# Turning the next routed tile's rows during the present tile, and dealing the sorted tiles out over three places of weights

## The chip, the cores and the metric

One core of a Trainium2 chip runs the whole program in one launch. The metric is the device time in microseconds (us); lower is better. Each time is that of one execution; the median of several is given.

## The reference, cut to what matters

The input is 64 sequences of 128 rows of 256 numbers (fp32). A state-space layer and a decayed cross attention, each followed by a layer norm, give rows x2. What matters here is the last part, a mixture of experts, and its layer norm:

```
shared = (silu(x Wg0) * (x Wu0)) Wd0                    # every row
probs  = sigmoid(x R + b); two experts of eight per row, scores s1, s2
out    = layernorm(x + shared + s1*expert_e1(x) + s2*expert_e2(x))
expert_e(x) = (silu(x Wg[e]) * (x Wu[e])) Wd[e]         # 256 -> 512 -> 256
```

There are 8192 rows, so 16384 pairs of a row and an expert. Which experts a row goes to depends on the data.

## The kernel before, in words

The rows are taken in 16 groups of 512. For each group, first_half (front and scan: the state-space layer), second_half (after: attention; route: the router) and the shared expert follow on each other. Work of different groups is interleaved by a planner that runs while the program is written: abreast (L1236) holds generators and always takes the step that is furthest behind; placed (L1254) gives a generator its place in time; a yielded number is the work of TensorE, in estimated us, that should pass before the generator goes on. work[0] counts that work (L535). The tile layer then orders each engine's instructions by readiness under these priorities, so an engine's order is fixed in the program, but need not be the order in which the source issues them.

**Routing.** route writes each row twice, with its destination and its score, into a table xs in HBM, in the region of its expert (indirect DMAs from GpSimd, POOL in the profile, L992). In five places tile_list (L1039) makes a list of tiles from the counts so far. BATCHES (L41) gives the number of tiles and rows: 9, 16, 16, 16 tiles of 256 rows after 4, 8, 12 and 16 groups, and 21 tiles of 128 rows at the end, 78 in all. The list is sorted by expert: position p of a batch holds the p-th tile of the sorted sequence. An entry holds the expert, the first row in xs, and a flag that says whether the expert differs from that of the tile three positions earlier.

**A routed tile.** There are three places of weights, routed_w0 to routed_w2 (1.5 MB each: gate, up and down of one expert); tile i uses place i % 3 (NW = 3). fetch (L1134) copies the list's entry (L1139, POOL), then SP reads it, loads the rows (rows_in, L1142) and, if the flag is set, the weights (L1148); the instruction waits for the place to be free and stands in SP's order also where it skips the transfer. SP carries many other DMAs in order. refill (L1121) fetches up to three tiles ahead; there[i] is the planned time at which tile i is ready, 12 us after its fetch.

one_tile (L1204) waits for there[i], runs hidden (L1156), then down (L1187) of the tile before, then refills. hidden transposes the rows on TensorE (four turns of 128 x 128 for 256 rows, two for 128), copies them from PSUM to rows_T on ScalarE (ACT, L1166), copies the row destinations `to` (L1168) and scores `wt` (L1170) on POOL, and yields 1.2. Then follow the products of gate and up in PSUM tiles gu (three buffers, shared with the shared expert), silu on ACT (L1182) and the multiply on VectorE (DVE, L1183) into hid: two rounds for 256 rows, one for 128. down makes the product with the third matrix, scales it (L1196) and scatters the rows to ys (L1197, indirect DMA of POOL; it reads `to`). The buffers: rows_in 3, rows_T 2, to and wt 3, hid 4, rows_out 2.

**The end.** After the last group the remaining tiles run (other_tiles, L1445), beside fill_behind (L1100), which writes filler rows behind each expert's region (8 indirect DMAs on POOL, 7 DMAs on SP, L1115), and the last shared expert. Then come the shared experts of seven groups and, for every group, combine: x2 plus the two rows of ys, layer norm, output.

All matmuls go through product (L536, the matmul at L543), transposes through turn (L545, L547), so the profile shows them under these lines, told apart by their tiles. One fp32 matmul shows as two MATMUL records, a transpose as one.

Of the kernel before, what the change touches and what calls it, by code (L numbers as in the profile page):

```python
# [11 lines left out]
F32 = mybir.dt.float32  # L12
AF = mybir.ActivationFunctionType
ALU = mybir.AluOpType
# [5 lines left out]
KD = D // P  # L20
# [7 lines left out]
NE = 8  # L28
# [8 lines left out]
NW = 3  # L37
# [3 lines left out]
BATCHES = [(4, 0, 9, 256), (8, 9, 16, 256), (12, 25, 16, 256), (16, 41, 16, 256), (16, 57, 21, 128)]  # L41
NT = sum(n for _, _, n, _ in BATCHES)
DX = D + 2
MOST = max(n for _, _, n, _ in BATCHES)
# [456 lines left out]
def shared_decay(K):  # L501

    with ExitStack() as ctx:
        _shared_decay(ctx, K)


def _shared_decay(ctx, K):  # L510
    tc, nc = K.tc, K.tc.nc
# [10 lines left out]
    const = ctx.enter_context(tc.tile_pool(name="masks", bufs=1))  # L522
# [12 lines left out]
    work = [0.0]  # L535

    def product(out, lhsT, rhs, **how):
        n = 1
        for size in rhs.shape[1:]:
            n *= size  # L540
        tiled = P // lhsT.shape[-1] if "tile_position" in how else 1
        work[0] += 2 * max(0.00084 * n, 0.11 if n > 64 else 0.06) / tiled
        nc.tensor.matmul(out, lhsT=lhsT, rhs=rhs, **how)  # L543

    def turn(out, src, ident):  # L545
        work[0] += 0.11
        nc.tensor.transpose(out, src, ident)  # L547
# [39 lines left out]
    def project(ps, w, col, src):  # L587

        for k in range(KD):
            product(  # L590
                ps, lhsT=w[:, k, col : col + P], rhs=src[:, k, :],
                start=(k == 0), stop=(k == KD - 1),
            )
# [445 lines left out]
    def tile_list(k):  # L1039

        groups, first, n, size = BATCHES[k]
        last = k == len(BATCHES) - 1
        d = done[k]
        pn = pm.tile([P, NE], F32, name="pm")
        product(pn, lhsT=ones, rhs=count, start=True, stop=True)
        if last:
            behind = small.tile([P, NE], F32, name="behind", bufs=1)
            nc.vector.tensor_tensor(behind, pn, behind0, ALU.add)  # L1050
            nc.vector.tensor_copy(behind_i, behind)

        def tiny(name, shape=(P, NE)):
            return small.tile(list(shape), F32, name=name, bufs=1)


        nt_f = tiny("nt_f")
        nc.vector.tensor_scalar(nt_f, pn, float(size - 1) if last else 0.0, None, ALU.add)
        nt_i = small.tile([P, NE], mybir.dt.int32, name="nt_i", bufs=1)
        nc.vector.tensor_copy(nt_i, nt_f)  # L1060
        nc.vector.tensor_scalar(nt_i, nt_i, size.bit_length() - 1, None, ALU.arith_shift_right)
        upto_e = tiny("upto_e")
        nc.vector.tensor_copy(upto_e, nt_i)
        nt = tiny("nt")
        nc.vector.scalar_tensor_tensor(nt, d, -1.0 / size, upto_e, ALU.mult, ALU.add)
        cum2 = tiny("cum2", (P, NE, NE))
        nc.vector.tensor_tensor(cum2, bef, nt.unsqueeze(1).to_broadcast([P, NE, NE]), ALU.mult)
        cum0 = tiny("cum0")
        nc.vector.tensor_reduce(cum0, cum2, AX.X, ALU.add)
        if not last:  # L1070
            more = tiny("more")
            nc.vector.tensor_scalar(more, cum0, -1.0, float(n), ALU.mult, ALU.add)
            nc.vector.tensor_scalar(more, more, 0.0, None, ALU.max)
            nc.vector.tensor_tensor(more, more, nt, ALU.min)
            nc.vector.scalar_tensor_tensor(done[k + 1], more, float(size), d, ALU.mult, ALU.add)
        cum = tiny("cum", (1, NE))
        nc.vector.tensor_tensor(cum, cum0[0:1], nt[0:1], ALU.add)

        skip = tiny("skip", (1, NE))
        nc.vector.tensor_scalar(skip, upto_e[0:1], -float(size), float(CAP), ALU.mult, ALU.add)  # L1080
        nc.vector.tensor_tensor(skip[:, 0 : NE - 1], d[0:1, 1:NE], skip[:, 0 : NE - 1], ALU.add)
        ge = small.tile([1, MOST, NE], F32, name="ge", bufs=1)[:, 0:n, :]
        nc.vector.tensor_tensor(
            ge, number[:, 0:n].unsqueeze(2).to_broadcast([1, n, NE]),
            cum.unsqueeze(1).to_broadcast([1, n, NE]), ALU.is_ge,
        )
        mine = ex[:, NW + first : NW + first + n]
        nc.vector.tensor_reduce(mine, ge, AX.X, ALU.add)
        nc.vector.tensor_scalar(mine, mine, float(NE - 1), None, ALU.min)
        nc.vector.tensor_tensor(ge, ge, skip.unsqueeze(1).to_broadcast([1, n, NE]), ALU.mult)  # L1090
        row = small.tile([1, MOST], F32, name="row", bufs=1)[:, 0:n]
        nc.vector.tensor_reduce(row, ge, AX.X, ALU.add)
        nc.vector.scalar_tensor_tensor(row, number[:, 0:n], float(size), row, ALU.mult, ALU.add)
        wh = what[:, first : first + n, :]
        nc.vector.tensor_scalar(wh[:, :, 0], mine, 1.0, None, ALU.add)
        nc.vector.tensor_scalar(wh[:, :, 1], row, d[0:1, 0:1], None, ALU.add)
        nc.vector.tensor_tensor(wh[:, :, 2], mine, ex[:, first : first + n], ALU.not_equal)
        known[0] = first + n
# [20 lines left out]
    ahead, room = [], [NW]  # L1119

    def refill():  # L1121

        while fetched[0] < min(room[0], known[0]):
            ahead.append(fetch(fetched[0]))
            there.append(work[0] + 12.0)
            fetched[0] += 1

    fetched, there = [0], []

    def shape(i):  # L1130

        return next((k, size) for k, (_, first, n, size) in enumerate(BATCHES) if i < first + n)
# [20 lines left out]

    listed, waiting = [0], []

    def hidden(i, t):  # L1156
        _, size = shape(i)
        w = weights[i % NW]
        wg = w[:, 0:SZ].rearrange("p (k i) -> p k i", k=KD)
        wu = w[:, SZ : 2 * SZ].rearrange("p (k i) -> p k i", k=KD)  # L1160
        ps = pm.tile([P, KD, size], F32, name="pm")
        for k in range(KD):
            for j in range(size // P):
                turn(ps[:, k, j * P : (j + 1) * P], t[:, j, k * P : (k + 1) * P], ident)
        tT = tiles.tile([P, KD, size], F32, name="rows_T", bufs=2)
        nc.scalar.copy(tT, ps)  # L1166
        to = tiles.tile([P, size // P], mybir.dt.int32, name="to", bufs=3)
        nc.gpsimd.tensor_copy(to, t[:, :, D])  # L1168
        wt = tiles.tile([P, size // P], F32, name="wt", bufs=3)
        nc.gpsimd.tensor_copy(wt, t[:, :, D + 1])  # L1170
        yield 1.2
        hid = []
        each = T // size
        for c0 in range(0, CF, each):
            psg = gu.tile([P, each, size], F32, name="gu")
            psu = gu.tile([P, each, size], F32, name="gu")
            for ps, w2 in ((psg, wg), (psu, wu)):
                for c in range(each):
                    project(ps[:, c, :], w2, (c0 + c) * P, tT)
                yield  # L1180
            hc = tiles.tile([P, each, size], F32, name="hid", bufs=4)
            nc.scalar.activation(hc, psg, AF.Silu)  # L1182
            nc.vector.tensor_tensor(hc, hc, psu, ALU.mult)  # L1183
            hid += [hc[:, c, :] for c in range(each)]
        return hid, to, wt

    def down(i, hid, to, wt):  # L1187
# [16 lines left out]
    def one_tile():  # L1204

        i = listed[0]
        listed[0] += 1
        refill()
        yield max(0.0, there[i] - work[0])
        made = yield from hidden(i, ahead.pop(0))  # L1210
        if waiting:
            yield from down(*waiting.pop())
        waiting.append((i, *made))

        room[0] = i + NW
        refill()
        yield
# [98 lines left out]
    for half in (L // 2, L // 4, L // 8):  # L1316
        t = const.tile([P, L // half, half], F32, name=f"middle{half}")
        n = L // half
# [6 lines left out]
    for side in range(2):  # L1325
        t = one.tile([P, KB // NS, NS], F32, name=f"half{side}", tag="dm")
# [3 lines left out]
        while half >= Q:  # L1330
# [7 lines left out]
        tT = const.tile([KB, P], F32, name=f"halfT{side}")  # L1338
# [4 lines left out]
    SZ = KD * FF  # L1343
# [6 lines left out]
                   allow_small_or_imprecise_dtypes=True)  # L1350
# [7 lines left out]
                   allow_small_or_imprecise_dtypes=True)  # L1358
# [8 lines left out]
    behind0 = const.tile([P, NE], F32, name="behind0")  # L1367
    nc.gpsimd.iota(behind0, pattern=[[CAP, NE]], base=0, channel_multiplier=1,
                   allow_small_or_imprecise_dtypes=True)
    number = const.tile([1, MOST], F32, name="number")  # L1370
    nc.gpsimd.iota(number, pattern=[[1, MOST]], base=0, channel_multiplier=0,
                   allow_small_or_imprecise_dtypes=True)
    done = [const.tile([P, NE], F32, name=f"done{k}") for k in range(len(BATCHES))]
    nc.vector.memset(done[0], 0.0)
    ex = const.tile([1, NW + NT], F32, name="ex")
# [3 lines left out]
    weights = []  # L1379
    for i in range(NW):  # L1380
        t = const.tile([P, 3 * SZ], F32, name=f"routed_w{i}")
# [4 lines left out]
                   allow_small_or_imprecise_dtypes=True)  # L1386
# [267 lines left out]
```

## Time and profile before

| | us |
|---|---|
| runs before: median (lowest to highest, 3) | 2053.07 (2049.54 to 2053.74) |
| the profiled execution | 2046.0 |
| its span | 2044.3 |

| group (line, engine, tiles) | instructions or records | busy us | mean ns |
|---|---|---|---|
| gate and up of routed tiles, 256 rows: L543 PE gu<-rows_T,routed_w | 1824 | 432.5 | 388 |
| the same, 128 rows | 672 | 78.7 | 275 |
| down of routed tiles: L543 PE pm<-routed_w,hid | 1080 | 258.4 | 383 |
| transposes of routed rows: L547 PE pm<-ident,rows_in | 270 | 42.4 | 273 |
| multiply of routed tiles: L1183 DVE | 135 | 92.3 | 686 |
| silu of routed tiles: L1182 ACT | 135 | 80.5 | 596 |
| scatter of routed rows: L1197 POOL | 135 | 138.4 | 1026 |

The whole moves 253.60 MB by DMA, and the granted TensorE clock is 0.984 of full. Busy time is the time in which an engine shows an instruction; a wait is idle time put down to what released the engine last, written "engine line <- releaser". PEld is TensorE's weight load, which overlaps its products. Routed tiles run from 380 us to about 1875 us of the span.

### The profile page before, as it was taken

To read this page: it belongs to the slowest core of one execution; us is meant where nothing else is said; L and a number is where in the kernel's file an instruction comes from. 1 tells how busy PE (TensorE), PEld (TensorE's weight loads), DVE (VectorE), ACT (ScalarE), POOL (GpSimd) and SP (SyncE) were. 2 spreads that over 40 slices of the span, in tenths; PEclk is the share of its full clock that TensorE was granted. 3 is DMA by queue.
4 is the path that set the end of the run, shared out by engine and by line. 5 is a ranking of instruction groups with operands and counts; after the bars stand their busy time and mean duration, and the time that the engine had idled before them with its cause. 6 is when DMAs were issued, how large, how long until landed. Compare 5 with 4: busy or idle time off the path is not lost. (4 is left out here: it accounts for less than half of the span.)

```text
span 2044.3 us, 26096 instructions
## 1 busy us (share of the span) xinstructions
PE 1894.9 (93%) x9252; PEld 1396.5 (68%) x9252; DVE 988.5 (48%) x2398; ACT 743.1 (36%) x1239; POOL 462.0 (23%) x697
## 2 busy tenths in 40 slices
PE   4989998999999999999999999998998999999996
PEld 2655666686767676777777676767676888886553
DVE  3667676565555564555555555554431111012574
ACT  3355344344343534353434252534121222221332
POOL 3030221221212122323223121222123222221110
PEclk9899999999999999999999999999999999999998
DMA  4011121422313234333333442433224555862772
GB/s 146 26 54 44 53 64 39 165 90 75 124 44 109 59 135 150 111 126 124 129 121 100 150 140 80 134 116 116 104 80 166 183 184 195 305 218 97 256 268 84
DMA packets 100629, 253.60 MB, mean 124 GB/s; under 512 B 22824, under 2 KB 60328, under 8 KB 91528
## 3 DMA queue, kind: packets, MB, share of 16 engines
q1 hardware_dynamic: 77368, 196.56, 29.1%
q0 software_dynamic: 17616, 52.46, 7.4%
q10 hardware_dynamic: 5504, 2.81, 0.5%
q8 instruction: 75, 1.23, 0.2%
q14 instruction: 66, 0.54, 0.1%
HBM read 207.33 MB, written 58.60 MB: 130 GB/s over the span
## 5 line engine op out<-in xcount | busy, mean ns | idle before, releaser
L543 PE MATMUL gu<-rows_T,routed_w 128*128 128x256 f32 (+1 forms) x2496 | 511.2, 358 | 40.3 <-ACT rows_T L1166 14.8
L543 PEld LDWEIGHTS gu<-rows_T,routed_w 128*128 128x128 f32 x2496 | 421.5, 193 | 115.8 <-issue 34.1
L1183 DVE TENSOR_TENSOR hid<-hid,gu 128x512 f32<-128x512 f32 x135 | 92.3, 686 | 389.4 <-PE gu L543 370.5
L543 PE MATMUL pm<-routed_w,hid 128*128 128x256 f32 x1080 | 258.4, 383 | 9.9 <-DVE hid L1183 9.9
L543 PE MATMUL pm<-xnT,w_in_s 128*128 128x512 f32 x512 | 243.4, 600 | 3.2 <-ACT xnT L580 3.1
L543 PE MATMUL gu<-x2T,shared_w 128*128 128x512 f32 x512 | 230.5, 596 | 3.5 <-DVE hc L1016 2.6
L543 PEld LDWEIGHTS pm<-routed_w,hid 128*128 128x128 f32 x1080 | 198.6, 190 | 51.3 <-DVE hid L1183 14.7
L1197 POOL DMA_INDIRECT ys<-rows_out,to x135 | 138.4, 1026 | 325.5 <-ACT rows_out L1196 252.4
L562 POOL TENSOR_TENSOR rstd<-var,mhalf 128x4 f32<-128x4 f32 x64 | 68.2, 1066 | 508.7 <-DVE mv L558 282.7
L628 DVE SCALAR_TENSOR_TENSOR xc<-pm,cw,xc 128x508 f32<-128x508 f32 (+2 forms) x192 | 141.2, 740 | 77.9 <-ACT xc L623 74.3
L543 PEld LDWEIGHTS gu<-x2T,shared_w 128*128 128x128 f32 x512 | 94.6, 190 | 111.5 <-issue 99.6
L1182 ACT ACTIVATE hid<-gu 128x512 f32<-128x512 f32 x135 | 80.5, 596 | 237.6 <-PE gu L543 217.4
L543 PEld LDWEIGHTS pm<-xnT,w_in_s 128*128 128x128 f32 x512 | 95.6, 193 | 87.2 <-issue 74.1
L567 ACT ACTIVATE x<-x,shift,rstd 128x256 f32<-128x256 f32 x132 | 72.6, 591 | 183.1 <-DVE shift L564 183.1
L543 PE MATMUL pm<-w_out_s,sz 128*128 128x256 f32 x512 | 122.0, 391 | 9.3 <-DVE sz L784 8.3
L1196 ACT ACTIVATE rows_out<-pm,wt 128x256 f32<-128x256 f32 x135 | 57.7, 469 | 199.0 <-PE pm L543 148.5
L543 PE MATMUL gu<-shared_w,hc 128*128 128x256 f32 x512 | 116.7, 382 | 7.3 <-DVE hc L1016 7.3
L543 PEld LDWEIGHTS pm<-w_out_s,sz 128*128 128x128 f32 x512 | 98.5, 195 | 32.9 <-DVE sz L784 14.1
L543 PEld LDWEIGHTS gu<-shared_w,hc 128*128 128x128 f32 x512 | 95.4, 190 | 26.9 <-DVE hc L1016 11.1
L992 POOL DMA_INDIRECT xs<-x,index x64 | 66.9, 1045 | 138.3 <-issue 75.4
L781 DVE SCALAR_TENSOR_TENSOR xc<-xc,dsk,pm 128x512 f32<-128x512 f32 x64 | 47.2, 744 | 84.5 <-PE pm L543 56.3
L623 ACT ACTIVATE xc<-pm,cb,cw 128x512 f32<-128x512 f32 x64 | 49.7, 777 | 105.1 <-PE pm L543 105.1
(233 smaller groups left out, 2465.6 us busy)
## 6 DMA issues: line engine op xcount, KB each, us to landing
routed_w<-in_ffn_dram SPq DMA_DIRECT2D x78, 1536.0 KB
picked<-ys SPq DMA_DIRECT2D x16, 1024.0 KB
rows_in<-xs SPq DMA_DIRECT2D x57, 258.0 KB
cT<-in_ctxT_dram POOLq DMA_DIRECT2D x16, 512.0 KB
cq<-chunks SPq DMA_DIRECT2D x16, 512.0 KB
x_rows<-x SPq DMA_DIRECT2D x16, 512.0 KB
xt<-in_x_dram POOLq DMA_DIRECT2D x10, 512.0 KB
xt<-x_rows SPq DMA_DIRECT2D x10, 512.0 KB
```

The lines of the kernel that those rows point to most:

```text
L543: nc.tensor.matmul(out, lhsT=lhsT, rhs=rhs, **how)
L562: nc.gpsimd.tensor_tensor(rstd, var, mhalf, ALU.pow)
L567: nc.scalar.activation(dst[:, b, :], src[:, b, :], AF.Identity, bias=shift[:, b : b + 1], scale=rstd[:, b : b + 1])
L623: nc.scalar.activation(xcf[:, c, :], ps, AF.Identity, bias=cb[:, c : c + 1], scale=cw[:, c, TAPS - 1 : TAPS],)
L628: nc.vector.scalar_tensor_tensor(xc[:, c, :, s:], ps3[:, :, : L - s], cw[:, c, TAPS - 1 - s : TAPS - s], xc[:, c, :, s:], ALU.mult, ALU.add,)
L781: nc.vector.scalar_tensor_tensor(y, xcf[:, c, :], dsk[:, c : c + 1], ps.rearrange("p b l -> p (b l)"), ALU.mult, ALU.add)
L992: s = nc.gpsimd.indirect_dma_start(out=xs, in_=rows[k][:, b, :], in_offset=None, out_offset=bass.IndirectOffsetOnAxis(ap=index[:, b, k : k ...
L1182: nc.scalar.activation(hc, psg, AF.Silu)
L1183: nc.vector.tensor_tensor(hc, hc, psu, ALU.mult)
L1196: nc.scalar.activation(y[:, j, :], ps[:, j, :], AF.Copy, scale=wt[:, j : j + 1])
L1197: s = nc.gpsimd.indirect_dma_start(out=ys, in_=y[:, j, :], in_offset=None, out_offset=bass.IndirectOffsetOnAxis(ap=to[:, j : j + 1], axis=0),)
```

## The change

Three things change.

The transposes, the copy to rows_T and the copies of `to` and `wt` become a function of their own, rows_turned. hidden of tile i calls it for tile i + 1 after the first round of its own products whose end finds tile i + 1 fetched and planned work within 8 us of there[i + 1] (so 4 us after its fetch), without a yield of its own. A tile whose rows are not turned by then does it itself as before.

The list deals the sorted tiles out: position p of a batch of n holds sorted tile p // 3 + (p % 3) * (n // 3) + min(p % 3, n % 3). So each of the three places of weights gets a contiguous run of the sorted sequence, where before it got every third tile. The flag still says whether the expert differs from that of three positions earlier.

For this the constant row `number` (0, 1, 2, ...) becomes one row for each batch size, made at the start by an iota on POOL and, for 16, two small DVE operations.

```diff
-            ge, number[:, 0:n].unsqueeze(2).to_broadcast([1, n, NE]),
+            ge, numbers[n].unsqueeze(2).to_broadcast([1, n, NE]),
...
-        nc.vector.scalar_tensor_tensor(row, number[:, 0:n], float(size), row, ALU.mult, ALU.add)
+        nc.vector.scalar_tensor_tensor(row, numbers[n], float(size), row, ALU.mult, ALU.add)
...
-    def hidden(i, t):
+    def rows_turned(i, t):
         _, size = shape(i)
-        w = weights[i % NW]
...
         nc.gpsimd.tensor_copy(wt, t[:, :, D + 1])
-        yield 1.2
+        turned_rows.append((tT, to, wt))
+
+    turned_rows = []
+
+    def hidden(i):
+        _, size = shape(i)
+        w = weights[i % NW]
...
+        if not turned_rows:
+            rows_turned(i, ahead.pop(0))
+            yield 1.2
+        tT, to, wt = turned_rows.pop()
         hid = []
...
             hid += [hc[:, c, :] for c in range(each)]
+            if ahead and not turned_rows and there[i + 1] - 8.0 <= work[0]:
+                rows_turned(i + 1, ahead.pop(0))
         return hid, to, wt
...
-        made = yield from hidden(i, ahead.pop(0))
+        made = yield from hidden(i)
...
-    number = const.tile([1, MOST], F32, name="number")
-    nc.gpsimd.iota(number, pattern=[[1, MOST]], base=0, channel_multiplier=0,
-                   allow_small_or_imprecise_dtypes=True)
+    numbers = {}
+    for n in sorted({n for _, _, n, _ in BATCHES}):
+        t = const.tile([1, -(-n // NW), NW], F32, name=f"number{n}")
+        nc.gpsimd.iota(t, pattern=[[1, -(-n // NW)], [n // NW, NW]], base=0, channel_multiplier=0,
+                       allow_small_or_imprecise_dtypes=True)
+        for s in range(1, NW):
+            if n % NW:
+                nc.vector.tensor_scalar(t[:, :, s], t[:, :, s], float(min(s, n % NW)), None, ALU.add)
+        numbers[n] = t.rearrange("p k s -> p (k s)")[:, 0:n]
```

More of the change, by code (lines that the diff above doesn't have):

```diff
@@ L1154, in _shared_decay @@
     listed, waiting = [0], []
-    def hidden(i, t):
+    def rows_turned(i, t):
         _, size = shape(i)
-        w = weights[i % NW]
-        wg = w[:, 0:SZ].rearrange("p (k i) -> p k i", k=KD)
-        wu = w[:, SZ : 2 * SZ].rearrange("p (k i) -> p k i", k=KD)
         ps = pm.tile([P, KD, size], F32, name="pm")
@@ L1170, in hidden @@
         nc.gpsimd.tensor_copy(wt, t[:, :, D + 1])
-        yield 1.2
+        turned_rows.append((tT, to, wt))
[3 more added lines that the diff above has]
+        w = weights[i % NW]
+        wg = w[:, 0:SZ].rearrange("p (k i) -> p k i", k=KD)
+        wu = w[:, SZ : 2 * SZ].rearrange("p (k i) -> p k i", k=KD)
+        if not turned_rows:
+            rows_turned(i, ahead.pop(0))
+            yield 1.2
+        tT, to, wt = turned_rows.pop()
         hid = []
```

## The prediction

> **What bounds the kernel now.** I read the page's busy table, then the stages, then in each stage who TensorE waited for, then the timeline at one place of each kind.
>
> ```profile
> PE 1894.9 (93%) x9252; PEld 1396.5 (68%) x9252; DVE 988.5 (48%) x2398; ACT 743.1 (36%) x1239; POOL 462.0 (23%) x697
> ```
>
> TensorE is busy 93% of the span and runs a fixed order, so its idle time is what can be won: 2044.3 - 1894.9 = 149 us. By stage (stretch, length, then PE, PEld, DVE, ACT, POOL busy, clock, DMA share, GB/s):
>
> ```profile
> 380.00:1500.00 1120.00, 1063.89 (x5314) 794.86 (x5313) 589.84 (x1413) 448.19 (x731) 263.15 (x352) 0.99 0.34 111
> 1500.00:1600.00 100.00, 87.97 (x385) 69.08 (x384) 23.61 (x86) 18.28 (x34) 30.79 (x54) 0.96 0.40 139
> 1600.00:1740.00 140.00, 139.91 (x665) 121.15 (x664) 17.87 (x26) 31.91 (x65) 30.47 (x66) 0.99 0.53 180
> 1740.00:1880.00 140.00, 129.06 (x905) 115.77 (x904) 15.11 (x22) 31.04 (x67) 33.81 (x82) 1.00 0.56 199
> ```
>
> Routed tiles run in these four; idle is 56, 12, 0 and 11 us. A (380-1500) has tiles between the layers, B (1500-1600) the list's end with the filling of rows, C the 256-row tiles alone, D the 128-row tiles. TensorE's waits (us, times, longest) in A:
>
> ```profile
> PE gu L543 <- ACT rows_T L1166: 14.8, 16, 3.2
> PE gu L543 <- ACT hid L1182: 11.5, 7, 1.8
> PE pm L543 <- DVE sz L784: 8.1, 7, 1.4
> ```
>
> in B, and in D:
>
> ```profile
> PE gu L543 <- DMA routed_w<-in_ffn_dram: 9.4, 3, 4.2
> ```
> ```profile
> PE pm L543 <- DVE hid L1183: 9.9, 17, 0.6
> PE gu L543 <- DMA routed_w<-in_ffn_dram: 1.0, 1, 1.0
> ```
>
> Weights stall TensorE 13.3 us in all: their traffic is nearly hidden already.
>
> **What the change moves.** The two kernels' instruction orders show it.
>
> *Transposes.* Same count (270 at 42.4/270 = 0.157 us), only moved. In A nearly every tile's transposes now stand 7 to 32 us of TensorE work ahead of its first gate product (work counted by the groups' mean durations); before, 27 tiles had under 2.5 us. Only the first tiles of later batches keep about 2 us. So of 14.8 us I take 12.8 away. No row load is then late: the last TensorE work that a rows load's issue depends on lies over 20 us of work ahead of the transposes in A (about 12 at batch starts), 9.5 in D; the loads land 1.7 to 7.7 us after issue, by the trace's packets.
>
> *ACT's queue.* One stall per four tiles looks like this:
>
> ```profile
> 798.47 1.28 ACT L693 ACT_TABLE_LOAD   x1
> 800.47 1.28 ACT L698 ACT_TABLE_LOAD   x1
> 802.49 1.28 ACT L1182 ACT_TABLE_LOAD   x1
> 803.78 0.60 ACT L1182 ACTIVATE hid<-gu 128x512 f32<-128x512 f32 x1
> 804.43 1.99 PE L543 MATMUL gu<-rows_T,routed_w 128*128 128x256 f32 x8 [1.83 <-ACT hid L1182]
> ```
>
> The silu that frees the gate's PSUM sat behind three table loads. In the new order it stands ahead of the softplus's three loads. Six such stalls are 11 us; I take 10. The 8.1 on sz came where a tile's hid multiply stood between the third and fourth sz pair on DVE; now it stands before the third: take 6.5.
>
> Against that: the new program has 9 more table loads (97 for 88). The row says 1283 ns each: 9 x 1.28 = 11.5 us of ACT. The Trainium skill (ScalarE: Activation LUTs, "What ACT_TABLE_LOAD costs") adds a drain of about 1380 ns, 2.66 us a switch: 24 us. The trace denies the drain here: the load at 798.47 ends at 799.75 and the next activation starts at 799.76. Bounds on TensorE 0 and 11.5; before, 11.5 us of stalls stood against 88 x 1.28 = 113 us of loads, a tenth, so 1.2. Transposes of bcs have 1.9 us of cover instead of 3.1 in seven groups (0 to 4; take 2, since a 0.5 us copy fits unless ACT is busy).
>
> *POOL.* Each tile's to and wt copies move a tile ahead. The copy of to waits for the scatter whose index buffer it takes (235.5 us in 55 waits before, up to 6.2 each), and POOL waits with it. It stood within one instruction of that scatter 20 times, now 56. Behind it wait the next list entry for SP, sometimes a layer norm's rstd. Bounds 0 and 28 (rival below), take 3: the order puts mostly list entries there, which SP needs later. And since other chains (norm, scan) then get less of TensorE's pauses, a fifth of the 29.3 won comes back: 6. A: -12.8 - 10 - 6.5 + 1.2 + 2 + 3 + 6 = -17.
>
> *Dealing.* From the counts of tokens per expert that the inputs give, 69 tiles fetched weights (the trace's packets: 70 loads of 128 x 12,288 B with the shared one); now 39. 30 x 1.57 = 47 MB fewer, 253.6 to 206 MB. Weights are still fetched for the first three tiles of each batch, where A's 2.8 us sit: no gain there. In B the three stalls are tiles 41 (4.2), 43 (2.3) and 44 (2.9). 44 no longer fetches. But on POOL two scatters now stand ahead of the last row scatters that 41's rows wait for: 2 x 1.26 = 2.5 later. 43's load has one filling less before it on SP but its product comes 4 us earlier: +1. Tile 45 stands on SP behind four fillings, which POOL releases between scatters: +2.5. B: -2.9 + 2.5 + 1 + 2.5 = +3, bounds -9 and +10.
>
> C has no idle; a load's window there shrinks from 13 to 10.9 us, and it lands in 6.5 to 7.7. Zero.
>
> *D.* The scheduler already put the next transposes ahead; what moves is the down product:
>
> ```profile
> 1789.34 0.69 DVE L1183 TENSOR_TENSOR hid<-hid,gu 128x512 f32<-128x512 f32 x1 [5.73 <-PE gu L543]
> 1790.08 1.99 PE L543 MATMUL pm<-routed_w,hid 128*128 128x256 f32 x8 [0.63 <-DVE hid L1183]
> 1791.91 3.73 PE L543 MATMUL gu<-rows_T,routed_w 128*128 128x128 f32 x32
> 1792.10 0.33 SPq L1148 DMA_DIRECT2D routed_w<-in_ffn_dram  x1
> ```
>
> Before: gate and up, transposes, own down, which waits 0.63 for its hid. Now the previous tile's down follows, so these 9.9 us go. The price: SP issues a tile's load when the down three tiles back ends (0.03 us after, above). That leaves two periods before, only one now, 6.41 - 0.63 = 5.78 us. A load lands 6.3 to 6.8 us after issue and the product starts 0.3 to 0.8 later: about 1.1 us of stall for each load. The skill (DMA: Bandwidth & Descriptors, "Anatomy of one DMA", a fit for GpSimd's queue) would give 2.0 + 1.573 MB / 436 GB/s = 5.6 us: no stall. The measured row decides. Of the nine loads in the last batch the first two have longer windows (a 256-row down lies in them); 7 x 1.1 = 7.7. D: -9.9 - 1.0 + 7.7 = -3, bounds -11 and +5.
>
> *Rest.* Two more iotas on POOL and two small DVE adds at the start, queued behind the masks that TensorE waits for: +0.5, nothing if the first norm covers them. The list's operations keep their shapes and number, so they cost nothing new. The closing stage (1880 on) is unchanged.
>
> Sum: -17 + 3 + 0 - 3 + 0.5 = -16.5 us. The profiled execution took 2046.0 (span 2044.3 and 1.7 around it), giving 2029.5; the median of the runs is 7.1 above it, 2053.07, giving 2036.6.
>
> **Rivals.** (1) *More is won* (0.14): A's 29.3 stay won and POOL and bcs cost nothing, in B only 44's stall changes, and half of D's new stalls are hidden since fewer loads share the DMA engines: -28 in A (table loads kept), -3 in B, -7 in D, +0.5: -37.5, 2015.5. For it: DMA traffic falls by a fifth.
> (2) *No change* (0.14): pauses only move. The norm and scan chains have their own length, and each pause taken away shows up before the next product: A gives 0, B (+3) and D (-3) cancel: 2053. For it: TensorE is at 95% in A already. Against: its waits for these chains (mk 4.4, x 3.8, cj 3.3) are small. That the transposes are not moved would end here too, but the order shows them moved.
> (3) *Slower* (0.22): POOL's queue. Where a to copy stands right behind its own scatter with an rstd among the next three instructions (3 places before, 8 now), the norm waits up to 5.6 us for the landing, then needs about 2.1 (rstd 1.07 and the small steps), against the 4.2 us of TensorE work that the planner places there: 3.5 each, 8 x 3.5 = 28. On the sum: -16.5 + 28 = +11.5, 2065. A place stalls at all once its wait exceeds 2.1 us, and the whole turns measurably slower once the eight lose 20 us, that is at waits of 4.7; the trace's are 4.0 to 6.2. Against: the gathered cover is often more than the planned 4.2, and three of the eight are there already.
>
> **Numbers.** The forecast -16.5 has 0.50. About 0.2% (4 us) is what measuring can tell: faster 0.64, same 0.14, slower 0.22. The range takes in B's and D's bounds and most of the rivals: 2015 to 2062.
>
> **What would show it.** Right: waits on rows_T in A near 2, on hid (ACT) near 1.5, on sz under 2; DVE hid in D gone and routed_w there near 7 to 8; 39 loads of routed weights in the packets; DMA 206 MB. Wrong: rstd waits growing with PE waits on x or cj; B's weights wait over 15; a new wait of TensorE on rows_in; A's idle still near 56.

## The result, and the profile after

The changed kernel took 2029.9 us (median of 4 runs, 2024.94 to 2034.3), the kernel before 2053.4 beside it: ratio 0.9889, 95% interval 0.9866 to 0.9912, or -23.5 us. The profiled execution took 2031.0 us, 15.0 less than that of before; the forecast was -16.5, and 2036.6 for the median. The profiled execution of before (2046.0) was shorter than every timed one (2049.54 to 2056.0), so the stages below account for 15.0 of the 23.5 us. All this holds for this comparison. In other sessions (one session is a set of kernels run side by side on one chip) the kernel before took 2014 to 2017 us, and there the changed kernel is not faster. Both are explained below as far as the runs go.

The page's busy line of the changed kernel:

```profile
PE 1887.0 (93%) x9252; PEld 1402.0 (69%) x9252; DVE 990.6 (49%) x2400; ACT 757.6 (37%) x1248; POOL 466.7 (23%) x699
```

By stages cut at the same instructions in both traces (A from the first gate product of a routed tile to the list's last count, then to the gate product of tile 46, of tile 57, and to the last one), before and after:

| stage | length | TensorE idle in it |
|---|---|---|
| A, between the layers | 1146.8 to 1131.0 | 56.1 to 44.7 |
| B, list's end and filling | 94.0 to 94.0 | 12.0 to 13.5 |
| C, 256-row tiles alone | 119.6 to 118.6 | 0.1 to 0 |
| D, 128-row tiles | 132.4 to 131.7 | 10.9 to 11.0 |
| behind D | 171.7 to 173.0 | 22.9 to 23.6 |

Line numbers are those of the kernel that ran: the copy to rows_T, the copy of `to`, silu, the multiply and the scatter are L1163, L1165, L1191, L1192 and L1208 in the changed kernel (L1166, L1168, L1182, L1183 and L1197 in the one before). TensorE's waits in A after the change (us, times, longest):

```profile
PE pm L543 <- ACT xnT L580: 9.1, 2, 5.0
PE pm L543 <- DVE mk L968: 7.9, 4, 3.3
PE pm L543 <- DVE cj L745: 6.1, 1, 6.1
PE pm L543 <- DVE sel L949: 6.0, 4, 3.4
PE pm L543 <- DVE dlb L725: 5.8, 4, 1.6
PE pm L543 <- DVE sz L784: 3.5, 5, 0.8
...
PE pm L543 <- ACT rows_T L1163: 1.7, 2, 0.8
```

The three waits that the change was to remove are nearly gone: rows_T 14.8 to 1.7, hid behind ACT 11.5 to none, sz 8.1 to 3.5. In their place stand waits on the norm (xnT), on routing (sel, mk) and on the scan (dlb, cj). They are fewer and longer: 15 of them make 34.9 us, 2.3 each, where the old three made 34.4 us in 30, 1.1 each. Their length matters for the clock, as the experiments show.

In B, and in D:

```profile
PE pm L547 <- DMA rows_in<-xs: 8.9, 2, 5.2
PE gu L543 <- DMA routed_w<-in_ffn_dram: 4.6, 1, 4.6
```
```profile
PE gu L543 <- DMA routed_w<-in_ffn_dram: 10.9, 7, 4.0
```

DMA moved 206.40 MB for 253.60, in 40 loads of 12,288-byte packets (39 and the shared one) for 70.

### The profile page after: what moved, and what is told of

Same layout as the page of the kernel before. It is cut to its first block, busy times and chain, and to the rows that moved or that the text cites. A ratio compares the mean times of both kernels' runs of the same rounds, so it can differ in the third digit from the quotient of the medians.

```text
span 2029.2 us, 26056 instructions
## 1 busy us (share of the span) xinstructions
PE 1887.0 (93%) x9252; PEld 1402.0 (69%) x9252; DVE 990.6 (49%) x2400; ACT 757.6 (37%) x1248; POOL 466.7 (23%) x699
## 2 busy tenths in 40 slices
DMA packets 96308, 206.40 MB, mean 102 GB/s; under 512 B 22344, under 2 KB 59848, under 8 KB 91048
## 5 line engine op out<-in xcount | busy, mean ns | idle before, releaser
L543 PE MATMUL gu<-rows_T,routed_w 128*128 128x256 f32 (+1 forms) x2496 | 504.4, 355 | 15.6 <-DMA routed_w<-in_ffn_dram 15.5
L1192 DVE TENSOR_TENSOR hid<-hid,gu 128x512 f32<-128x512 f32 x135 | 92.5, 685 | 395.9 <-PE gu L543 327.6
L1208 POOL DMA_INDIRECT ys<-rows_out,to x135 | 138.2, 1024 | 380.7 <-ACT rows_out L1207 327.4
L1191 ACT ACTIVATE hid<-gu 128x512 f32<-128x512 f32 x135 | 80.4, 596 | 152.1 <-PE gu L543 135.7
L543 PE MATMUL pm<-w_out_s,sz 128*128 128x256 f32 x512 | 117.0, 382 | 4.3 <-DVE sz L784 3.8
L640 ACT ACTIVATE sz<-pm 128x512 f32<-128x512 f32 x64 | 37.9, 594 | 113.1 <-PE pm L543 113.1
```

Source lines behind the costliest of these rows:

```text
L640: nc.scalar.activation(sz[:, c, :], ps, AF.Silu)
L1208: s = nc.gpsimd.indirect_dma_start(out=ys, in_=y[:, j, :], in_offset=None, out_offset=bass.IndirectOffsetOnAxis(ap=to[:, j : j + 1], axis=0),)
```

## The experiments

My theory was that the gain is made between the layers by the order of the queues, the rival that fewer loads make it, another that pauses only move. "Half clock" is the time in the trace's clock record at which TensorE was granted half speed; its cost is the excess of the matmuls in it over the mean of the same shape outside.

### First session: one part alone, and two suspects

In turn only, the rows of numbers are plain again; deal only is the kernel before with the dealt numbers.

```diff
 turn only
-        nc.gpsimd.iota(t, pattern=[[1, -(-n // NW)], [n // NW, NW]], base=0, ...
+        nc.gpsimd.iota(t, pattern=[[NW, -(-n // NW)], [1, NW]], base=0, ...
-        for s in range(1, NW): ...
 deal only (from before)
-            ge, number[:, 0:n].unsqueeze(2).to_broadcast([1, n, NE]),
+            ge, numbers[n].unsqueeze(2).to_broadcast([1, n, NE]),
 fourth buffer
-        to = tiles.tile([P, size // P], mybir.dt.int32, name="to", bufs=3)
+        to = tiles.tile([P, size // P], mybir.dt.int32, name="to", bufs=4)
-        wt = tiles.tile([P, size // P], F32, name="wt", bufs=3)
+        wt = tiles.tile([P, size // P], F32, name="wt", bufs=4)
 own down in the last batch
-            if ahead and not turned_rows and there[i + 1] - 8.0 <= work[0]:
+            if ahead and not turned_rows and i + 1 < BATCHES[-1][1] and there[i + 1] - 8.0 <= work[0]:
```

Turn only:

> The transposes a tile ahead, the list in its sorted order as before (69 weight loads, 15 of 21 in the last batch). Theory (the gain is the order of the queues between the layers): that stage keeps its idle near 45 us and its waits on rows_T, hid and sz stay under 4 us each; in the 128-row stage 13 loads instead of 7 have the short window, at the 10.9/7 = 1.55 us that a stall took there, so about 20 us of waits for weights, 9 more than the changed kernel has, and 2 to 5 more at the list's end: about 2042, 12 us over the changed kernel and still faster than before. Rival (the gain is the 47 MB fewer): between the layers the idle goes back to 56 us, and with the last batch's stalls it is slower than before, about 2060.

Deal only:

> The kernel before with the dealt list alone (39 weight loads). Theory: only tile 44's stall of 2.9 us and the 1.0 us in the 128-row stage go: 2049, -4 us or 0.2%, idle between the layers still 55 to 57 us, waits on rows_T, hid and sz there 34 us as before. Rival (traffic): most of the 23 us are won here, 2035 or less, and those three waits shrink with the traffic.

Fourth buffer:

> The changed kernel with a fourth buffer for to and wt, so that a tile's copies wait for the scatter of one tile further back; only POOL's order changes. If the 19 us of waits that came up in place of the three that went (on xnT, sel, mk, dlb, cj between the layers) stem from POOL standing at to: the wait of to falls from 160 us to under 60, POOL's rstd waits and those of DVE on rstd shrink, and 5 to 15 us are won: 2015 to 2025. If they are the chains' own length: to's wait falls as much and the time stays within 3 us of 2030.

Own down:

> The changed kernel, except that in the last batch (128-row tiles) no tile's transposes are turned inside the tile before, so that there each tile's down product follows its own gate and up, as before. Theory: the 10.9 us of waits for weights there fall to 1 or 2 since the window is two periods again, and the 9.9 us on hid come back: the stage's length is the same within 2 us, 2029 in all. Rival: the stalls there are from loads that collide with rows and scatters whatever the window, and stay near 8 with hid's 10 on top: 2038.

The kernel before took 2016.6 us here. Turn only: 2038.4, ratio 1.0105 (1.0079 to 1.0131), slower by 21.8 where I had expected a gain. Deal only: 2003.6, 0.9947 (0.9930 to 0.9963). Fourth buffer: 2011.0, 0.9979 (0.9967 to 0.9991). Own down: 2016.7, 0.9995 (0.9980 to 1.0010). So my theory fell here: the transposes ahead cost time and the fewer loads won it. In own down the last stage is 131.0 us, with 9.9 of waits on hid and none on weights; the changed kernel had 131.7, with 10.9 on weights. That trade is as I had it. With the fourth buffer POOL's wait of to for its scatter fell to 34 us (156.8 in the changed kernel of the next session), but DVE's wait on rstd stayed (81.3 us; 80.4 there). Against the changed kernel's ratio of that session, 1.0017, the fourth buffer wins 0.4% or 8 us, from ratios of two sessions.

### Second session: both kernels again, and hardly any loads

```diff
 few loads (in both kernels: the later batches load no weights)
-        nc.vector.tensor_tensor(wh[:, :, 2], mine, ex[:, first : first + n], ALU.not_equal)
+        nc.vector.tensor_tensor(wh[:, :, 2], mine, mine if first else ex[:, first : first + n], ALU.not_equal)
```

Before again:

> The kernel before once more, for its profile beside those of the runs of this call and the last, where the kernel before took 2016.6 us. There the dealt list alone gave -10.7 us where I had put -4, and the early transposes alone +21 where I had put -11. The theory that the order of the queues wins is therefore in doubt; a new one: the transposes ahead win nothing, the fewer loads do. With it the profile of before in that setting has about 40 us of idle between the layers and 34 us of waits on rows_T, hid and sz there as in the first profile. Ratio to before 1 within 0.1%.

After again:

> The changed kernel once more beside before. If the -1.1% is the change's in every setting: ratio 0.989. If the three kernels near it are a guide (fourth buffer 0.998, own down in the last batch 0.9995): 0.997 to 1.001, and the first result held for its setting alone.

Before, few loads:

> The kernel before without the weight loads of every batch but the first (it leaves them out, so the later tiles compute with wrong weights): 9 loads for 69, 94 MB less, order and everything else as before. New theory (loads cost through traffic): faster than the dealt list alone, which left out 30: -15 to -25 us. Rival (only TensorE's own waits for weights cost): those of the first profile, 13 us at most, -13.

After, few loads:

> The changed kernel without the weight loads of every batch but the first (left out as in the kernel before this one). The difference to that kernel is then that of the transposes' place alone, with hardly any loads: theory of the queues' order: 10 to 17 us faster than it. New theory (transposes ahead win nothing, the pauses only move): within 5 us of it, or slower.

Before took 2013.7 us (2012.3 as its own entry, 0.9995). The changed kernel took 2016.0: 1.0017 (1.0007 to 1.0027), slower by 0.2%. Without later loads: before 1980.5, 0.9840 (0.9827 to 0.9854), and after 1978.7, 0.9833 (0.9816 to 0.9851), equal within their intervals. The loads cost more than either expectation had it: 33.1 us in before, of which TensorE's own waits for weights are 15.2 (before again). Before again has 37.3 us of idle in A, near the 40 expected, but 23.5 of waits on rows_T, hid and sz for the expected 34: the one on sz is gone.

So in these two sessions what the early transposes do depends on the loads. With 69 loads they cost 1.05%, with 39 they cost 0.70% (1.0017 less 0.9947, of two sessions), with 7 to 9 nothing. By stages, one profile of each kernel: in A they add 24.0 us with 69 loads, 9.3 with 39 and still 5.4 with 7 to 9; in D they add 5.5, take off 0.9, and take off 13.8. So with few loads it is D that makes up for A. Stage A:

| kernel | loads | length of A | idle | half clock, its cost | rest |
|---|---|---|---|---|---|
| before, first profile | 69 | 1146.8 | 56.1 | 20.5, 9.5 | 1081.2 |
| after, first profile | 39 | 1131.0 | 44.7 | 34.1, 14.4 | 1071.9 |
| before again | 69 | 1113.2 | 37.3 | 0, 0 | 1075.9 |
| after again | 39 | 1116.9 | 34.7 | 34.1, 13.9 | 1068.3 |
| deal only | 39 | 1107.6 | 32.1 | 3.4, 1.6 | 1073.9 |
| turn only | 69 | 1137.2 | 45.2 | 58.0, 24.0 | 1068.0 |
| before, few | 9 | 1099.8 | 27.0 | 0, 0 | 1072.8 |
| after, few | 7 | 1105.2 | 29.6 | 20.5, 7.7 | 1067.9 |

"Rest" is the length less idle and half-clock cost; A holds the same 5455 records of TensorE in every kernel. Every kernel with early transposes has 5 to 9 us less in its products (rest), and in these two sessions 8 to 24 us of half-clock cost, where the kernels without have 0 to 1.6. The page's clock column shows it too. The stretch 700 to 1000 us (length, PE, PEld, DVE, ACT, POOL busy, clock, DMA share, GB/s) of before again, deal only, after again and turn only:

```profile
700.00:1000.00 300.00, 287.71 (x1538) 221.93 (x1536) 167.79 (x412) 131.18 (x213) 78.38 (x109) 1.00 0.40 131
```
```profile
700.00:1000.00 300.00, 289.21 (x1539) 224.10 (x1538) 172.37 (x421) 132.21 (x217) 78.84 (x111) 1.00 0.33 107
```
```profile
700.00:1000.00 300.00, 283.95 (x1513) 220.16 (x1512) 168.12 (x407) 135.22 (x217) 81.70 (x111) 0.98 0.34 110
```
```profile
700.00:1000.00 300.00, 278.35 (x1418) 214.85 (x1416) 158.91 (x402) 126.19 (x204) 76.38 (x107) 0.96 0.38 124
```

Compare the clock column: 1.00 without early transposes, with 69 loads and with 39, and 0.98 and 0.96 with them. (The first profile of before has 0.99 here.) The counts of matmuls are not compared, since the same stretch holds different work in each.

How loads come into it is seen on DVE. DVE does the scan's multiplication with cq (L752), for which it waits on a 512 KB DMA; everything behind it on DVE waits too, the routing's sel and mk among it. The wait in before again, deal only, before with few loads, and turn only:

```profile
DVE eq L752 <- DMA cq<-chunks: 12.3, 7, 3.2
```
```profile
DVE eq L752 <- DMA cq<-chunks: 6.4, 3, 3.4
```
```profile
DVE eq L752 <- DMA cq<-chunks: 0.5, 1, 0.5
```
```profile
DVE eq L752 <- DMA cq<-chunks: 19.1, 7, 3.8
```

Fewer loads, fewer such waits; after again has 6.9 us in 3, like deal only. In turn only each is longer (19.1/7 = 2.7 us for 1.8), and TensorE waits there for

```profile
PE pm L543 <- DVE sel L949: 14.6, 4, 4.3
PE pm L543 <- DVE mk L968: 14.3, 5, 4.8
```

which is 28.9 us, where after again has 14.9 (6.8 and 8.1). Group by group the two waits go together. Take the seven groups from 800 us on in turn only, after, after again and after few, 28 in all. In 14 of them DVE waited for cq, and 4 to 8 us later TensorE began a pause of 1.8 to 4.8 us for sel or mk; in the 14 others that pause was 0.2 to 1.0 us. In before again DVE waited for cq in all seven, and TensorE's pauses for mk were four of 1.1 us: the old order hid most of it. So the early transposes pass DVE's waits on to TensorE. That the weights' bytes delay cq is inferred from the order of the four kernels above; no run moved cq alone.

One long pause does not hang on the loads: that of about 6 us for cj near 715 us, with one of 3.2 us behind it. It stands in every kernel with early transposes between the layers (3.5 us in slot copy on POOL, below), and brings 13.7 of the 20.5 us of half clock in after few.

### Third and fourth session: can the cost be mended

```diff
 slot copies later
-        nc.vector.tensor_copy(rows[0][:, :, D], slot[:, g * GB : (g + 1) * GB])
-        nc.scalar.copy(rows[1][:, :, 0 : D + 1], rows[0][:, :, 0 : D + 1])
...
         nc.vector.reciprocal(tot, tot)
+        nc.vector.tensor_copy(rows[0][:, :, D], slot[:, g * GB : (g + 1) * GB])
+        nc.scalar.copy(rows[1][:, :, 0 : D + 1], rows[0][:, :, 0 : D + 1])
 late turn
-            if ahead and not turned_rows and there[i + 1] - 8.0 <= work[0]:
+            if ahead and not turned_rows and i + 1 > BATCHES[-1][1] and there[i + 1] - 8.0 <= work[0]:
 slot copy on POOL
-        nc.vector.tensor_copy(rows[0][:, :, D], slot[:, g * GB : (g + 1) * GB])
+        nc.gpsimd.tensor_copy(rows[0][:, :, D], slot[:, g * GB : (g + 1) * GB])
```

Slot copies later, then late turn, and late turn with a fourth buffer for to and wt:

> The changed kernel, with the two copies that write the slot numbers into a layer's rows issued further down on DVE and ACT, behind the steps that make the weights (TensorE's, POOL's and SP's orders stay the same). In the changed kernel the first of them stood on DVE for 7.15 us, waiting for a store of 512 KB issued 8 us before, at one place; TensorE then paused 6.4 and 3.2 us, and its clock was halved for 13.7 us. Theory (a wait that the new order put on DVE, plus half clock behind the pause): that pause falls under 3 us, the half clock there to 3.4 us or nothing: -7 to -12 us against the changed kernel, so a ratio to before of 0.996 to 0.998. Rival (the pause is the chain's own length and the clock costs nothing): ratio 1.0 to 1.002.

> The dealt list, and transposes turned a tile ahead only in the last batch (128-row tiles, from its second tile on): between the layers the order of before, in the last stage that of the changed kernel. If the early transposes cost between the layers and not in the last stage: the stage before as with the dealt list alone (half clock under 20 us, waits on cq 3 times), the last stage 126 to 131 us, ratio 0.993 to 0.995. If they win in the last stage what the loads don't take: up to 0.992.

> The kernel of the run before with a fourth buffer for to and wt. In the changed kernel that made the last stage 126.1 us instead of 130.0 by the profiles of two different runs; if it is POOL's wait for its scatter that holds back rows there, it is 2 to 5 us faster than the run before (ratio 0.991 to 0.993); if the difference was chance, the two agree within 2 us.

Slot copy on POOL, in the fourth session:

> The changed kernel, with the copy of the slot numbers into a layer's rows made by POOL instead of DVE (orders of TensorE, ACT and SP unchanged; the run that issued it later on DVE left it at the same place, with 6.7 us of waiting). On POOL it stands behind two scatters that end when the store has landed. Theory (a wait that the new order put on DVE, plus half clock behind the pause): DVE's wait of 7 us and TensorE's on cj of 6.0 to 6.4 us go, the 13.7 us of half clock there too, 7 to 12 us less than the changed kernel: ratio to before 0.996 to 0.998 where before takes 2014, 0.983 to 0.986 where it takes 2052. Rival (the chain's own length; another wait takes its place): the same ratio as the changed kernel, 1.0017 or 0.989.

The place that both slot edits aim at, in the changed kernel of the second session:

```profile
701.00 0.55 SPq L1031 DMA_DIRECT2D x_rows<-x  x1
...
709.18 0.17 DVE L965 COPY x<-slot 128x4 f32<-128x4 f32 x1 [7.15 <-DMA x_rows<-x]
...
712.02 0.68 DVE L745 TENSOR_TENSOR cj<-cj,eb 128x512 f32<-128x512 f32 x1
...
712.85 0.55 PE L543 MATMUL pm<-cj,bj 128*128 128x128 f32 x1 [6.42 <-DVE cj L745]
```

A copy of 0.17 us held DVE for 7.15, since it writes into a buffer that a store still reads; cj stood behind it. In before again cj (713.3) ran ahead of that copy, the store was issued at 715.9, and the copy followed at 720.7 without a wait: the store had landed 3.2 us after its issue, where in after again it took 8.2.

In the third session before took 2051.1 us, as in the first comparison. Slot copies later: 2033.8, 0.9920 (0.9899 to 0.9941). The edit did not do what it was for: at this place DVE still waited 6.7 us, A is 1131.0 us as in the first profile of after, and nothing is won on that kernel's 0.9889. Late turn: 2038.5, 0.9939 (0.9916 to 0.9961), in the expected range. With the fourth buffer: 2027.6, 0.9884 (0.9860 to 0.9907), 10.9 us faster where I had expected 2 to 5; by the profiles 6.2 of it are in D and 4.2 in A. In D these two show what POOL's wait does (late turn first; the second kernel has four buffers):

```profile
POOL to L1165 <- DMA ys<-rows_out,to: 54.4, 18, 6.2
...
PE gu L543 <- DMA routed_w<-in_ffn_dram: 11.1, 5, 4.2
```
```profile
PE gu L543 <- DMA routed_w<-in_ffn_dram: 7.9, 6, 1.6
POOL to L1165 <- DMA ys<-rows_out,to: 5.7, 2, 4.7
```

D is 131.7 and 125.5 us. The longest stall for weights, 4.2 us at tile 59, goes: behind the waiting to stands the copy of the list entry from which SP takes the next load; 59's load followed 58's by 10.0 us with three buffers and by 7.8 with four. The pair after again and fourth buffer has 130.0 and 126.1.

Fourth session: before 2046.8, slot copy on POOL 2020.8, 0.9887 (0.9861 to 0.9914). DVE's wait went and TensorE's on cj fell from 6.1 (first profile of after) to 3.5, but the pause on mk behind it grew from 3.2 to 4.0, and half clock at the place is 10.2 us as it was in that profile. The ratio is that of the changed kernel, 0.9889: no gain can be measured, and the rival (another wait takes its place) stands.

## Why the prediction came out, and where it did not

*A, -17.* Measured -15.8 in the comparison it was made for, and the cause holds there: late turn has the dealt list without early transposes between the layers, and its A is 1145.6 us, so the transposes make 14.6 and the dealing 1.2 (single profiles of two sessions). The runs agree: late turn's 0.9939 less the changed kernel's 0.9889 is 0.5%, 10 us, with 3.5 lost in B (below). The removed waits were right in sum: 12.8 + 10 + 6.5 = 29.3 forecast, 13.1 + 11.5 + 4.6 = 29.2 measured. What came back was mis-sized. I had 12.2 for table loads, bcs, POOL and "a fifth of the 29.3"; idle fell by only 11.4, so 17.8 came back as other pauses, the shares of which I can't separate. Two terms were absent from the sum. Half clock cost 4.9 more (9.5 to 14.4), and the products themselves took 9.3 less (rest, 1081.2 to 1071.9). Of this, 9.0 is in the products that come first after a pause, shorter pauses than the listed ones included: there were 67 outside half clock before and 34 after, and each adds 0.2 us over the median of its shape, as it overlaps with no product ahead of it. So a pause taken away was worth its length and 0.2 us more. -11.4 + 4.9 - 9.3 = -15.8. The total is near the forecast partly by luck: more came back as pauses than I had, half clock cost more, and the third term offset most of both.

Elsewhere the same terms are -2.6 + 13.9 - 7.6 = +3.7 (before again to after again). The third rival's sign came true there, not its mechanism. It had POOL's to delaying rstd; DVE's wait on rstd did grow (64.2 to 80.5 us in all), but with the fourth buffer it stayed at 81.3, so to did not cause it. In the sum above the largest term is the half clock behind longer pauses, which I did not have. My second rival, that pauses only move, is nearly right of the idle there: 2.6 us less.

*POOL in A, +3.* The fourth buffer's A is 3.9 us shorter than after again's: the right size, in two sessions' single profiles. But its idle is 0.8 us longer; what falls is the half-clock time, from 34.1 to 23.9 us. That POOL's wait made this is not shown.

*B, +3.* Measured 0. Tile 44's stall went, as forecast. But TensorE now waits 8.9 us for rows (the new wait I had named as a sign of being wrong), where it had waited 4.2 for tile 41's weights. I had 2.5 for the later rows of tile 41; those of 41 and 42 cost 3.7 and 5.2. Late turn's B is 90.5 us and has no wait for rows, so the dealing won 3.5 and the early transposes lost 3.5.

*D, -3.* Measured -0.7 in length. The 9.9 on hid went and the loads' price was 10.9 for 7.7: seven stalls as forecast, mean 1.6 us instead of 1.1. The step that failed is "about 1.1 us of stall for each load": it fits six of the seven (6.9 us), but left out the stall of 4.0 at tile 59, which came from POOL's to (1.5 in late turn with the fourth buffer). With few loads D is 130.9 us in the old order and 117.1, free of idle, in the new one, so the order is worth 14 us there and the loads take nearly all of it.

*C and the rest.* C is 1.0 us shorter (0 forecast); the start came 1.1 us later and the stage behind D took 1.3 more (+0.5 forecast for both). ACT has the 9 more instructions, and the wait on bcs in A is 0.8 us for the 2 I had put.

*Dealing.* 39 loads and 206 MB as forecast. That the fewer loads win nothing in A does not hold where before takes 2014 to 2017: deal only's A is 5.6 us shorter than before again's, and its gain of 0.53% in all (10.7 us by the ratio) is more than the 4 I expected. My price of a load counted TensorE's own waits for weights alone; here DVE's waits for cq fell by 5.9 us (12.3 to 6.4), and I had no term for them.

*What stays open.* The kernel before, unchanged, took 2047 to 2053 us in three sessions and 2014 to 2017 in two, and the change won 1.1% in the first kind and nothing in the second; the changed kernel itself ran once in each. The chip's number on record does not tell the two kinds apart: 9 stands for a session of each. What tells the profiles apart is when results of TensorE reach their reader. In the six profiles of the slower kind 11 to 21 waits of ACT, DVE and POOL ended only when TensorE's signal came, over 0.5 us after the product's end (as the profile models it), 13 to 25 us in all; in the eight others none did. Before, first profile, and before again, at one place ("remote": the trace shows no releaser close enough):

```profile
536.40 0.60 PE L547 MATMUL pm<-ident,rows_in 128*128 128x128 f32 x4
...
540.10 0.59 ACT L1166 COPY rows_T<-pm 128x512 f32<-128x512 f32 x1 [1.98 <-remote]
```
```profile
541.42 0.60 PE L547 MATMUL pm<-ident,rows_in 128*128 128x128 f32 x4
...
542.35 0.59 ACT L1166 COPY rows_T<-pm 128x512 f32<-128x512 f32 x1
```

The copy starts 3.1 us after the transposes end in the first and 0.3 in the second. Late turn, run in the third session, is late at the same place of the program. The weights landed equally fast (7.10 and 7.09 us from issue, mean of 69 loads). An early transpose takes such a delay off the path, which fits the change winning there. But in before's A this one, 3.1 us, is the only late signal for rows_T, and A's change differs by 19.5 us between the two kinds (-15.8 and +3.7). No run tested it, and the cause is open. Nor was deal only run where before takes 2050, or late turn with four buffers where it takes 2014; so whether one version beats both kernels everywhere is open. Where both were run, deal only beats both (0.9947 against 1 and 1.0017); in the other kind, late turn with four buffers equals the changed kernel (0.9884 and 0.9889).

## What to carry to other kernels

Before moving work ahead of an in-order engine, ask what the pauses will look like afterwards: many of 1 to 2 us can cost less than a few of 3 to 6, because the latter also take TensorE's clock. Ask too whose waits the moved work had been hiding: here those of DVE for cq. A load that never stalls TensorE itself can still cost; here, as far as the runs show, through a DMA that another engine waits for. Repeat both kernels in another session before trusting a gain of 1%: here the sign changed.

## What the runs showed of the hardware

Pauses of TensorE go with half clock from about 2 us on. In the routed part (380 to 1880 us) of the 14 profiles, half clock stood in the pause or within 5 us behind it for 11 of 202 pauses between 0.8 and 2 us, for 20 of 28 between 2 and 3 us, for 35 of 42 between 3 and 4 us, and for all of 40 longer ones (in 11 of these last 75 cases it had begun before the pause). A period lasted 3.4 us or a multiple (3.4, 6.8, 10.2, 13.7), and matmuls in it took twice as long (41.6 us busy, 20.6 of it excess, in the changed kernel). The Trainium skill (TensorE: Matmul & The Clock Gate, "HAM oscillation") puts the limit of a pause at about 3.4 us, but here 2 us were often enough. Its free-running window of 3413 ns ("What's actually happening") agrees with the lengths of the periods.
